# Side work of VectorE moved to other places of the iteration, two GpSimd operations behind a third, and the last stores cut by planes

## The chip, the cores and the metric

The kernel runs on one core of a Trainium2 chip. The metric is the device time of one execution in microseconds (us), as the median of three runs; lower is better. One execution was profiled besides, and the trace of it gives every instruction of the engines: TensorE (PE, its weight loads shown apart as PEld), VectorE (DVE), ScalarE (ACT), GpSimd (POOL) and SyncE (SP), which only issues DMAs here.

## The reference

A residual block of four modulated one-dimensional convolutions over x of 128 samples, 64 channels and 1024 positions, all in float32. For each sample and layer the weights are scaled by a style vector and normalised:

```python
def _layer(x, style, w, b, mw, mb, typ):
    s = style @ mw.T + mb
    weight = SCALE * w * s[:, None, :, None]
    demod = lax.rsqrt(jnp.sum(weight * weight, axis=(2, 3)) + EPS)
    weight = weight * demod[:, :, None, None]
    if typ == 'same':
        out = jax.vmap(_conv_same)(x, weight) + b[None, :, None]
    elif typ == 'upsample':
        out = jax.vmap(_conv_up)(x, weight.transpose(0, 2, 1, 3)) + b[None, :, None]
        out = _blur(out, 2.0 * blur_k, (1, 1))
    elif typ == 'downsample':
        xb = _blur(x, blur_k, (2, 2))
        out = jax.vmap(_conv_down)(xb, weight) + b[None, :, None]
    return out
...
for i, typ in enumerate(('same', 'upsample', 'same', 'downsample')):
    out = _layer(out, style, weights[i], biases[i], mod_w[i], mod_b[i], typ)
return x + out
```

## The kernel before

**The idea.** The four layers are linear in x, so for each sample they are one convolution of nine taps, a bias and a few samples at both ends that are computed apart. The kernel builds the composed weights of each sample on TensorE and then applies them with a fast algorithm: the nine taps are three groups of three, and the positions are stored as three planes (position modulo 3), so that five products of plane combinations with weight combinations give the three output planes.

**Groups and iterations.** The samples are taken four at a time: 32 groups, `NQ = 32`. The loop over `q` is a software pipeline; iteration q works on four groups at once: on q (its last products and its outputs), on n = q + 1 (its first products), on c = q + 2 (the last stages of its weights, its inputs) and on s = q + 3 (the first stage of its weights). All instructions are issued in the order written; each engine takes its own in that order, and semaphores hold back what is not ready.

**Weights.** `scale3`, `stage1` (split in `stage1_a` and `stage1_b`), `stage2` and `stage3` build the composed weights through the PSUM tiles psS, psR and psW. Each result is copied to SBUF by ScalarE with a factor per sample from a table: S with tB or tBn, R with tC, Wf with t0, wd with tA. Two parts of S are added up by VectorE from PSUM (L422), and GpSimd adds one part of S to another (L425, "the addition into S"). `combine_a` and `combine_b` form the weight combinations H from Wf on VectorE, SBUF to SBUF; between them `residual` adds the residual path, with the table t3.

**Inputs and products.** VectorE forms from X, the loaded planes, the tile G (`in_g01`, `in_g2`), then T3 (`in3`) and both T0 and T4 (`in04`); GpSimd forms T1 (`in1`, L566) and T2 (`in2`, L571) from G. TensorE makes the five products in `conv0` to `conv4`, twelve matmuls each, which the trace records as 24; conv0 to conv3 go into psA and conv4 into Y. `copy_m3` (ScalarE), `sum1` and `sum2` (VectorE, from PSUM) put them together between the products: sum1 reads psA behind conv1, and conv2 may only then write on in psA; sum2 reads psA behind conv2 and writes Y, and only then conv4 of the next iteration may add to Y. `output` scales a plane with td and adds tb, on ScalarE; `store` sends the planes from SP.

The order of VectorE in an iteration before the change is: sum2, combine_a, combine_b, T0/T4, T3, G, sum1, the additions into S, side work. That of GpSimd: T1, the addition into S, T2, side work. That of TensorE: psR, conv4, psW, conv3, psW, conv0 (first third), conv1 (first third), a slot or psS, conv1, conv0, psS, conv0, conv2. psR is thus the first work of an iteration.

**Side work.** The modulation of the samples beyond the first ones, their tables, the constants of the bias and the ends of the sequence are spread over the iterations by hand. `SLOTS` names the iterations in which TensorE makes a product for them, into psE, which ScalarE copies to `raw` ("slot iterations": 1, 2, 3, 5, 6, 7 small ones, and 9, 12, 14, 19, 24 with twelve matmuls for the ends); there `stage1_a` comes later. `EXTRA` names what follows on VectorE and GpSimd, by iteration and place: `var_root`, `var_inverse` (a reciprocal) and `var_newton` make the normalisation, `table_*` the tables, `vector_*` and `const_rest` the constants, `setup*`, `rest*` and `blur_side` the ends. Before the change both places, 0 and 1, are in the same spot, behind the additions into S.

**Buffers.** X and the T tiles have two buffers, G one, the weight tiles three or four; PSUM has two tiles for psA, one tile for psS, psR, psW and psE together, and one for Y.

Of the kernel before, what the change touches and what calls it, by code (L numbers as in the profile page):

```python
# [55 lines left out]
K = 3  # L56
# [7 lines left out]
def kernel(  # L64
# [9 lines left out]
    nc = tc.nc  # L74
    NP, P, NXC = x.shape
    B = 2 * NP
    NQ = B // 4
# [146 lines left out]
    def var_root(bs, src, ls=slice(0, NL)):  # L224
        src = by_layer(src, bs)[:, ls]
        nc_a.activation(nw[:, ls, bs], src, AF.Sqrt, bias=eps)
        nc_v.tensor_scalar(var[:, ls, bs], src, EPS, None, op0=ALU.add)
# [46 lines left out]
    def table_B(bs):  # L274
        table(nc_g, tB, bs, ALT, DOWN, sc[:, 2, bs], sc[:, 1, bs])

    def table_Bn(bs):
        qs = slice(bs.start // 4, bs.stop // 4)
        nc_g.tensor_scalar_mul(tBn[:, qs], tB[:, qs], -1.0)
# [429 lines left out]
    def vector_a1(bs):  # L709
        nc_g.tensor_mul(a1[:, bs], sc[:, 2, bs], sc[:, 1, bs])  # L710
# [318 lines left out]
    def var_and_constant(ps):  # L1029
# [11 lines left out]
        12: (ends1(0), HB * 5, HB * 5),  # L1041
        14: (ends1(1), HB * 4, HB * 4),
        19: (ends2, HB * 8, HB * 8),
        24: (ends3, HB * 3, HB * 3),
    }

    def after(side):
        return raw[turn[0]][:, side, :]

    def layers(i, j):  # L1050
        return REST, slice(i, j)
# [1 line left out]

    EXTRA = {
        (1, 1): lambda: const_rest(0, PART[1], after(0)),
        (2, 0): lambda: (table_B(REST), table_Bn(REST), vector_a1(REST)),
        (2, 1): lambda: (var_root(REST, after(0)), const_rest(1, PART[1], after(1))),
        (3, 0): lambda: (var_inverse(*layers(2, 3)), table_0(REST), vector_b1(REST)),
        (3, 1): lambda: (
            const_rest(2, PART[1], after(0)),  # L1060
            table_b(PART[1]),
            var_newton(*layers(2, 3)),
            var_inverse(*layers(1, 2)),
        ),
        (4, 0): lambda: (
            table_A(REST, dm[:, 2, REST]),
            var_inverse(*layers(0, 1)),
            var_newton(*layers(0, 2)),
            vector_c0(REST),
        ),  # L1070
        (4, 1): lambda: (table_C(REST), vector_c2(REST)),
        (5, 0): lambda: vector_Da(REST),
        (5, 1): lambda: (const_rest(0, REST, after(0)), var_inverse(*layers(3, 4))),
        (6, 0): lambda: (var_newton(*layers(3, 4)), table_3(REST), setup_x(0)),
        (6, 1): lambda: const_rest(1, REST, after(0)),
        (7, 0): lambda: setup_x(1),
        (7, 1): lambda: (const_rest(2, REST, after(0)), table_b(REST)),
        (8, 0): setup0,
        (9, 0): setup3,
        (9, 1): lambda: rest0(0),  # L1080
        (10, 0): lambda: rest0(1),
        (10, 1): lambda: setup1(0),
        (11, 0): lambda: setup1(1),
        (12, 1): lambda: rest1(0),
        (14, 1): lambda: rest1(1),
        (15, 0): lambda: rest1_bias(0),
        (16, 0): lambda: rest1_bias(1),
        (19, 1): lambda: rest2(0),
        (20, 0): lambda: rest2(1),
        (20, 1): lambda: blur_side(0, 0),  # L1090
        (21, 0): lambda: blur_side(1, 0),
        (21, 1): lambda: blur_side(0, 1),
        (22, 0): lambda: blur_side(1, 1),
        (22, 1): lambda: blur_side(0, 2),
        (23, 0): lambda: blur_side(1, 2),
        (24, 1): rest3,
        (25, 0): rest3_bias,
    }

    def extra(*at):  # L1100
# [2 lines left out]
    for q in range(NQ):  # L1103
        n, c, s = q + 1, q + 2, q + 3
        if q == 1:
            nc.sync.dma_start(Xe, x_ends)
        if q == 5:
            zeros()
        if n == NQ:
            conv4(q)  # L1110
            for i in range(2):
                output(q, 2, i)
            for i in range(2):
                output(q, 1, i, nc_v)
            for i in range(2):
                store(q, i, slice(1, 3))
            conv0(q, *range(K))
            for i, (eng, queue) in enumerate(zip(BOTH, (nc_a, nc.sync))):
                output(q, 0, i, eng)
                store(q, i, slice(0, 1), queue)  # L1120
            break
# [8 lines left out]
        if n == NQ - 1:  # L1130

            conv3(n, ps_w)
            copy_m3(n)
            conv4(q, 0, 1)
            for i in range(2):
                output(q, 1, i)
            conv1(n)
            sum1(n)
            conv4(q, 2)
            for i in range(2):  # L1140
                output(q, 2, i)
            in04(n, PAIR[0])
            in04(n, PAIR[1])
            conv0(q, 0)
            conv2(n)
            conv0(q, 1, 2)
            sum2(n)
            for i in range(2):
                output(q, 0, i)
                store(q, i)  # L1150
            continue

        conv4(q)
# [11 lines left out]
            stage3(c, 0)  # L1165
        conv3(n)
        copy_m3(n)
        in04(n)
        if q:
            in3(c)  # L1170
# [12 lines left out]
        if q:  # L1183
            in_g2(c)
            load(c + NX)
        later = q and c < NQ - 1
        if later:
            in1(c, nc_g)
        if n == NQ - 2:
            combine_a(n + 1, lambda: sum1(n))  # L1190
            combine_b(n + 1)
# [12 lines left out]
        conv2(n, 0)  # L1204
        if q in SLOTS:
            stage1_b(s)
        if later:
            in2(c, nc_g)
        extra(q, 0)
        extra(q, 1)  # L1210
        if s + 1 < NQ:
            scale3(s + 1)
        conv2(n, 1, 2)
# [86 lines left out]
```

## Time and profile before

| | us |
|---|---|
| median of 3 runs | 494.18 (494.17 to 494.41) |
| the profiled execution | 494.43 |
| its span, first to last instruction | 492.6 |
| granted TensorE clock, mean | 0.998 |
| PE busy | 480.1 |
| DVE busy | 406.0 |
| ACT busy | 290.3 |
| POOL busy | 141.9 |
| DMA, mean over the span | 143 GB/s |

The span is what the trace shows; the execution's own time is 1.8 us longer. Rows of a timeline give the start, the busy length, the engine, the line, the operation, what it writes and reads, its size, how many instructions were merged, and in brackets how long the engine was idle before and who ended that. A row of the chain of waits gives start, length and the instruction on the path that ended last. Adjoining operations of VectorE overlap by some 0.08 us in these records, and matmuls, whose ends are modelled, by some 0.2; the chain starts a group of matmuls at the end of the one before.

### The profile page before, as it was taken

What the parts mean: (1) busy time and instruction counts of PE and PEld (TensorE: products, weight loads), DVE (VectorE), ACT (ScalarE), POOL (GpSimd) and SP (SyncE); (2) the same over time, 40 slices, a digit from 0 to 9 for tenths busy, and PEclk for the clock granted to TensorE, in tenths of its full rate; (3) what the DMA queues carried; (4) which work ended last, traced back from release to release, by engine and by line L of the source; (5) the groups of instructions that cost most, each with busy time, mean ns of one, the idle gap of its engine ahead of it and who ended that gap; (6) DMA issues with size and microseconds to landing.
All of it is one profiled execution on the core that took longest, in us unless ns stands there. A gap on an engine that the chain in (4) does not pass through costs nothing.

```text
span 492.6 us, 22188 instructions
## 1 busy us (share of the span) xinstructions
PE 480.1 (97%) x10056; PEld 363.4 (74%) x10056; DVE 406.0 (82%) x632; ACT 290.3 (59%) x579; POOL 141.9 (29%) x175
## 2 busy tenths in 40 slices
PE   8999999999999999999999999999999999999995
PEld 6877787667767766777888888876777777777763
DVE  5986888898898969996769998759999869878783
ACT  5456646566556656556566656656566657556552
POOL 3544423434123232123232122232133332121200
PEclk9999999999999999999999999999999999999999
DMA  7220744442234442344532344442344442434224
GB/s 251 95 89 4 241 156 166 173 172 100 103 149 173 174 164 62 124 174 173 173 134 90 131 169 173 174 152 77 120 173 173 173 175 87 140 146 167 89 86 172
DMA packets 19727, 70.42 MB, mean 143 GB/s; under 512 B 2224, under 2 KB 2992, under 8 KB 19632
## 3 DMA queue, kind: packets, MB, share of 16 engines
q1 hardware_dynamic: 19408, 68.70, 38.4%
q8 instruction: 79, 1.29, 1.1%
q10 hardware_dynamic: 224, 0.29, 0.2%
q14 instruction: 16, 0.13, 0.1%
HBM read 35.36 MB, written 33.62 MB: 140 GB/s over the span
## 4 chain that ended last, share of the span: by engine, by line
PE 86%; DVE 9%; POOL 1%; issue 1%; ACT 1%; DVEq 0%
PE psA L593 40%; PE psW L480 14%; PE psR L439 12%; PE Y L593 11%; PE psS L369 5%; PE psE L823 2%; DVE Y L501 1%; DVE G L501 1%; PE Y L169 1%; DVE S L422 1%; ACT o L662 1%; DVE Ve L839 1%; PE Y L316 1%; DVE Ye L839 0%; DVE Ve L838 0%
## 5 line engine op out<-in xcount | busy, mean ns | idle before, releaser
L593 PE MATMUL psA<-T,H 64*64 64x340 f32 x2304 | 193.3, 446 | 0.6 <-DVE y L501 0.5
L593 PEld LDWEIGHTS psA<-T,H 64*64 64x64 f32 x2304 | 95.3, 133 | 51.1 <-issue 7.6
L566 POOL TENSOR_TENSOR T<-G 128x684 f32<-128x684 f32 x30 | 50.1, 1671 | 283.4 <-DVE G L501 251.5
L439 PE MATMUL psR<-S,E 64*64 64x192 f32 (+1 forms) x2304 | 87.6, 299 | 0.7 <-ACT S L340 0.4
L439 PEld LDWEIGHTS psR<-S,E 64*64 64x64 f32 x2304 | 80.8, 133 | 8.2 <-issue 1.0
L340 ACT ACTIVATE R<-psR,tC 128x448 f32<-128x448 f32 x63 | 36.6, 631 | 69.2 <-PE psR L439 67.4
L501 DVE SCALAR_TENSOR_TENSOR G<-X 128x1376 f32<-128x1376 f32 (+2 forms) x66 | 76.1, 1191 | 0.0
L593 PE MATMUL psA<-T,Wf 64*64 64x340 f32 x768 | 74.8, 447 | 0.0
L593 PE MATMUL Y<-T,Wf 64*64 64x340 f32 x768 | 62.2, 448 | 3.1 <-DVE Y L501 2.8
L340 ACT ACTIVATE Wf<-psW,t 128x384 f32<-128x384 f32 (+1 forms) x126 | 56.4, 498 | 12.2 <-PE psW L480 12.2
L480 PE MATMUL psW<-R,w0s 64*64 64x128 f32 (+1 forms) x1536 | 62.5, 287 | 0.4 <-ACT Wf L340 0.3
L501 DVE SCALAR_TENSOR_TENSOR y<-psA,m 128x680 f32<-128x680 f32 (+1 forms) x33 | 27.8, 845 | 37.8 <-PE psA L593 37.8
L480 PEld LDWEIGHTS psW<-R,w0s 64*64 64x64 f32 x1536 | 51.8, 133 | 7.8 <-ACT Wf L340 1.2
L662 ACT ACTIVATE o<-Y,tb,td 128x340 f32<-128x340 f32 x64 | 37.2, 631 | 27.7 <-ACT R L340 14.1
L571 POOL TENSOR_TENSOR T<-G 128x684 f32<-128x684 f32 x30 | 53.2, 1775 | 0.0
L580 DVE TENSOR_TENSOR T<-G 128x1368 f32<-128x1368 f32 (+1 forms) x33 | 50.5, 1534 | 0.0
L593 PEld LDWEIGHTS Y<-T,Wf 64*64 64x64 f32 x768 | 32.3, 133 | 20.9 <-DVE Y L501 6.0
L369 PEld LDWEIGHTS psS<-wd,w2n 64*64 64x64 f32 x1160 | 39.2, 133 | 10.3
L662 ACT ACTIVATE o<-psA,tb,td 128x340 f32<-128x340 f32 x63 | 36.7, 634 | 14.7 <-PE psA L593 14.7
L340 ACT ACTIVATE S<-psS,tBn 128x256 f32<-128x256 f32 x58 | 24.4, 471 | 25.7 <-PE psS L369 25.6
L625 ACT COPY m<-psA 128x680 f32<-128x680 f32 (+1 forms) x33 | 23.3, 710 | 25.6 <-PE psA L593 25.6
L662 ACT ACTIVATE o<-y,tb,td 128x340 f32<-128x340 f32 x62 | 38.1, 668 | 0.0
(147 smaller groups left out, 543.6 us busy)
## 6 DMA issues: line engine op xcount, KB each, us to landing
X<-in_x SPq DMA_DIRECT2D x64, 516.0 KB, 4.4
out<-o SPq DMA_DIRECT2D x62, 510.0 KB, 4.7
out<-o SPq DMA_DIRECT2D x2, 340.0 KB, 4.0
Xe<-in_x_ends SPq DMA_DIRECT2D x1, 512.0 KB, 7.9
par<-in_params SPq DMA_DIRECT2D x2, 192.0 KB, 3.4
par_s<-in_params_s SPq DMA_DIRECT2D x1, 196.0 KB, 2.7
par<-in_params SPq DMA_DIRECT2D x2, 96.0 KB, 2.7
out<-Oe SPq DMA_DIRECT2D x1, 192.0 KB, 3.1
```

The costliest lines, as they stand in the source:

```text
L340: nc_a.activation(dst, src, AF.Copy, scale=f)
L369: nc.tensor.matmul(ps[r][cols, at * C : (at + n) * C], weight[rows], wd[c if r == 0 else 1 - c][rows, taps], start=first, stop=last, skip_ ...
L439: nc.tensor.matmul(ps[r][cols, lo * C : (lo + m) * C], E[rows, e + 2, :], src[rows, a, :], start=(n == 0), stop=(n == 8), skip_group_check ...
L480: nc.tensor.matmul(ps[r][cols, at : at + m * C], w0s[kind][rows, k, :], rt[c][rows, first : first + K * (m - 1) + 1 : K, :], start=(n == 1 ...
L501: nc_v.scalar_tensor_tensor(out, x, f, y, op0=ALU.mult, op1=op)
L566: eng.tensor_add(t[:, :, 0, :NJ], plane(g, 2), plane(g, 1))
L571: eng.tensor_sub(t[:, :, 1, :NJ], plane(g, 2), plane(g, 1))
L580: nc_v.tensor_sub(t[:, pairs, :, :NJ], both(a, PL), both(b, 1))
L593: nc.tensor.matmul(ps[s][cols, :NB], w, Ts[q, tag][rows, c, i, g : g + NB], start=(g == 0 and m == 3), stop=(g == K - 1), skip_group_check ...
L625: nc_a.copy(m3c[q][:, s], a)
L662: nc_a.activation(dst, src, AF.Identity, bias=add, scale=d3)
L823: nc.tensor.matmul(ps[r][cols, : HB * n].rearrange("c (b j) -> c b j", j=n), weight(i, r, c)[rows], moving(i, r, c)[rows], start=(i == 0), ...
```

## The change

Three things are moved; apart from one `var_inverse` call that takes the place of two, no operation of the computation is added or left out.

1. The places 0, 1 and 2 of `EXTRA` are now at three spots: 0 ahead of T0/T4, 1 ahead of sum1 (in the last but one iteration ahead of combine_a), 2 where both were before, behind T2. All of VectorE's side work has gone to 0 and 1; tables and other GpSimd work that comes late stay at 2. The side work is also dealt out anew over the iterations, and slot 24 is now slot 25.
2. T1 (`in1`) is issued right ahead of T2, so on GpSimd both follow the addition into S.
3. In the last two iterations the stores are cut by planes: in iteration 30 planes 1 and 2 are stored ahead of plane 0; in iteration 31 plane 1 is made by VectorE ahead of conv4 in the issue order, and each plane has a store of its own, one of plane 1 and one of plane 0 from ScalarE's queue.

```diff
--- before.py
+++ after.py
@@ -1041,7 +1041,7 @@
         12: (ends1(0), HB * 5, HB * 5),
         14: (ends1(1), HB * 4, HB * 4),
         19: (ends2, HB * 8, HB * 8),
-        24: (ends3, HB * 3, HB * 3),
+        25: (ends3, HB * 3, HB * 3),
     }
 
     def after(side):
@@ -1053,48 +1053,37 @@
 
     EXTRA = {
         (1, 1): lambda: const_rest(0, PART[1], after(0)),
-        (2, 0): lambda: (table_B(REST), table_Bn(REST), vector_a1(REST)),
-        (2, 1): lambda: (var_root(REST, after(0)), const_rest(1, PART[1], after(1))),
-        (3, 0): lambda: (var_inverse(*layers(2, 3)), table_0(REST), vector_b1(REST)),
-        (3, 1): lambda: (
-            const_rest(2, PART[1], after(0)),
-            table_b(PART[1]),
-            var_newton(*layers(2, 3)),
-            var_inverse(*layers(1, 2)),
-        ),
-        (4, 0): lambda: (
-            table_A(REST, dm[:, 2, REST]),
-            var_inverse(*layers(0, 1)),
-            var_newton(*layers(0, 2)),
-            vector_c0(REST),
-        ),
-        (4, 1): lambda: (table_C(REST), vector_c2(REST)),
-        (5, 0): lambda: vector_Da(REST),
-        (5, 1): lambda: (const_rest(0, REST, after(0)), var_inverse(*layers(3, 4))),
-        (6, 0): lambda: (var_newton(*layers(3, 4)), table_3(REST), setup_x(0)),
-        (6, 1): lambda: const_rest(1, REST, after(0)),
-        (7, 0): lambda: setup_x(1),
-        (7, 1): lambda: (const_rest(2, REST, after(0)), table_b(REST)),
-        (8, 0): setup0,
-        (9, 0): setup3,
-        (9, 1): lambda: rest0(0),
-        (10, 0): lambda: rest0(1),
+        (2, 1): lambda: (const_rest(1, PART[1], after(1)), var_root(REST, after(0))),
+        (2, 2): lambda: (table_B(REST), table_Bn(REST), vector_a1(REST)),
+        (3, 0): lambda: (var_inverse(*layers(2, 3)), var_newton(*layers(2, 3))),
+        (3, 1): lambda: const_rest(2, PART[1], after(0)),
+        (3, 2): lambda: (table_b(PART[1]), table_0(REST), vector_b1(REST)),
+        (4, 0): lambda: (table_A(REST, dm[:, 2, REST]), var_inverse(*layers(0, 2))),
+        (5, 0): lambda: (var_newton(*layers(0, 2)), vector_c0(REST)),
+        (5, 1): lambda: const_rest(0, REST, after(0)),
+        (5, 2): lambda: (table_C(REST), vector_c2(REST), vector_Da(REST)),
+        (6, 0): lambda: (var_inverse(*layers(3, 4)), var_newton(*layers(3, 4))),
+        (6, 2): lambda: table_3(REST),
+        (7, 0): lambda: const_rest(1, REST, after(0)),
+        (7, 1): lambda: const_rest(2, REST, after(0)),
+        (7, 2): lambda: (table_b(REST), zeros()),
+        (8, 0): lambda: (setup_x(0), setup_x(1)),
+        (9, 0): lambda: (setup0(), setup3()),
+        (10, 0): lambda: rest0(0),
         (10, 1): lambda: setup1(0),
-        (11, 0): lambda: setup1(1),
-        (12, 1): lambda: rest1(0),
-        (14, 1): lambda: rest1(1),
-        (15, 0): lambda: rest1_bias(0),
-        (16, 0): lambda: rest1_bias(1),
-        (19, 1): lambda: rest2(0),
-        (20, 0): lambda: rest2(1),
-        (20, 1): lambda: blur_side(0, 0),
-        (21, 0): lambda: blur_side(1, 0),
-        (21, 1): lambda: blur_side(0, 1),
-        (22, 0): lambda: blur_side(1, 1),
-        (22, 1): lambda: blur_side(0, 2),
-        (23, 0): lambda: blur_side(1, 2),
-        (24, 1): rest3,
-        (25, 0): rest3_bias,
+        (11, 0): lambda: rest0(1),
+        (11, 1): lambda: setup1(1),
+        (13, 0): lambda: rest1(0),
+        (15, 0): lambda: rest1(1),
+        (16, 0): lambda: rest1_bias(0),
+        (17, 0): lambda: rest1_bias(1),
+        (20, 0): lambda: rest2(0),
+        (21, 0): lambda: rest2(1),
+        (22, 0): lambda: (blur_side(0, 0), blur_side(1, 0)),
+        (23, 0): lambda: (blur_side(0, 1), blur_side(1, 1)),
+        (24, 0): lambda: (blur_side(0, 2), blur_side(1, 2)),
+        (26, 0): rest3,
+        (27, 0): rest3_bias,
     }
 
     def extra(*at):
@@ -1104,16 +1093,14 @@
         n, c, s = q + 1, q + 2, q + 3
         if q == 1:
             nc.sync.dma_start(Xe, x_ends)
-        if q == 5:
-            zeros()
         if n == NQ:
+            for i, queue in enumerate((nc.sync, nc_a)):
+                output(q, 1, i, nc_v)
+                store(q, i, slice(1, 2), queue)
             conv4(q)
             for i in range(2):
                 output(q, 2, i)
-            for i in range(2):
-                output(q, 1, i, nc_v)
-            for i in range(2):
-                store(q, i, slice(1, 3))
+                store(q, i, slice(2, K))
             conv0(q, *range(K))
             for i, (eng, queue) in enumerate(zip(BOTH, (nc_a, nc.sync))):
                 output(q, 0, i, eng)
@@ -1139,6 +1126,7 @@
             conv4(q, 2)
             for i in range(2):
                 output(q, 2, i)
+                store(q, i, slice(1, K))
             in04(n, PAIR[0])
             in04(n, PAIR[1])
             conv0(q, 0)
@@ -1147,7 +1135,7 @@
             sum2(n)
             for i in range(2):
                 output(q, 0, i)
-                store(q, i)
+                store(q, i, slice(0, 1))
             continue
 
         conv4(q)
@@ -1165,6 +1153,7 @@
             stage3(c, 0)
         conv3(n)
         copy_m3(n)
+        extra(q, 0)
         in04(n)
         if q:
             in3(c)
@@ -1183,9 +1172,7 @@
         if q:
             in_g2(c)
             load(c + NX)
-        later = q and c < NQ - 1
-        if later:
-            in1(c, nc_g)
+        extra(q, 1)
         if n == NQ - 2:
             combine_a(n + 1, lambda: sum1(n))
             combine_b(n + 1)
@@ -1204,10 +1191,10 @@
         conv2(n, 0)
         if q in SLOTS:
             stage1_b(s)
-        if later:
+        if q and c < NQ - 1:
+            in1(c, nc_g)
             in2(c, nc_g)
-        extra(q, 0)
-        extra(q, 1)
+        extra(q, 2)
         if s + 1 < NQ:
             scale3(s + 1)
         conv2(n, 1, 2)
```

## The prediction

> **What bounds the kernel now.** I read the page first, then the chain of waits, then the timeline of single engines. Times are us from the span's start.
>
> ```profile
> span 492.6 us, 22188 instructions
> PE 86%; DVE 9%; POOL 1%; issue 1%; ACT 1%; DVEq 0%
> ```
>
> TensorE sets the end; VectorE stands on the chain for 9%. An iteration begins with the products into psR, so the distance from one psR to the next is its length (rows of the chain, two of a group of matmuls, one of a wait):
>
> ```profile
> 285.75 2.50 PE psR L439 x72
> 299.90 2.50 PE psR L439 x72
> 77.97 2.50 PE psR L439 x72
> 166.54 2.50 PE psR L439 x72
> 211.90 2.50 PE psR L439 x72
> 314.04 2.50 PE psR L439 x72
> 360.03 2.50 PE psR L439 x72
> 175.89 1.94 PE psE L823 x24
> 323.40 2.60 PE psE L823 x24
> L731 PE MATMUL psE<-cc,wsum 64*64 64x16 f32 (+1 forms) x16 | 1.1, 217 | 0.0
> 196.64 1.89 DVE Ye L839
> PEld Y L593 <- DVE Y L501: 6.0, 9, 1.1
> ```
>
> An undisturbed iteration takes 299.90 - 285.75 = 14.15. Iterations 3 to 8 take 88.57: six of 14.15 (84.90), four small slots of four matmuls each at 1.1/16 x 4 = 0.28 (1.1), and 2.6 more. Iterations 9 to 11 take 45.36 = 42.45 + 1.94 of slot + 1.0. Iterations 19 to 21 take 45.99 = 42.45 + 2.60 + 0.9. These **4.5 us** are conv4 waiting for sum2 (the weight load of Y waits 9 times for VectorE's Y), and in front of sum2 the chain shows side work such as Ye at 196.64.
>
> **What the moves save.** In the new order nothing but the two additions into S stands on VectorE between sum1 and sum2, so sum2 waits for TensorE alone, as here (sum2 at 314.09, 0.05 behind psR):
>
> ```profile
> 311.07 0.87 DVE L501 SCALAR_TENSOR_TENSOR y<-psA,m 128x680 f32<-128x680 f32 x1 [1.82 <-PE psA L593]
> 312.11 1.94 PE L593 MATMUL psA<-T,H 64*64 64x340 f32 x24
> 314.09 0.87 DVE L501 SCALAR_TENSOR_TENSOR Y<-m,psA 128x680 f32<-128x680 f32 x1 [1.64 <-PE psA L593]
> 60.12 0.80 PE L593 MATMUL psA<-T,H 64*64 64x340 f32 x8 [0.29 <-DVE y L501]
> 59.12 0.86 DVE L501 SCALAR_TENSOR_TENSOR y<-psA,m 128x680 f32<-128x680 f32 x1
> ```
>
> I count all 4.5 as saved. The floor is nothing, if what moves comes back in front of sum1.
>
> **What they cost in front of sum1.** Cover there is VectorE's idle 1.82 before sum1, plus 0.08 that adjoining operations overlap: 1.9. Beyond it conv2 waits at once: in iteration 1 conv2 starts 0.14 behind sum1's end (59.98 to 60.12), and in the steady one sum1's end 311.94 + 0.14 is 0.03 short of conv2 at 312.11. A slot iteration has about the same cover (1.8 to 1.9: sum1 comes earlier, but a longer group stands ahead of conv2); those with a psE of L823 have its 1.9 to 2.6 besides.
>
> The price of each operation where it ran undisturbed (its duration less 0.08 that the next one overlaps, plus 0.03 before one that needs its result):
>
> ```profile
> 92.39 0.37 DVE L759 TENSOR_TENSOR oc<-raw,dm 128x16 f32<-128x16 f32 x1
> 92.94 0.25 DVE L236 TENSOR_TENSOR nw<-dm,var 128x96 f32<-128x96 f32 x1
> 93.69 0.74 DVE L230 RECIPROCAL dm<-nw 128x96 f32<-128x96 f32 x1
> 183.58 0.56 DVE L838 TENSOR_TENSOR Ye<-raw,a 128x384 f32<-128x384 f32 x1
> 198.45 0.74 DVE L799 SCALAR_TENSOR_TENSOR g<-par,g 128x192 f32<-128x192 f32 x2
> 331.89 0.69 DVE L839 TENSOR_TENSOR Ve<-Ve,c 128x512 f32<-128x512 f32 x1
> ```
>
> A reciprocal costs 0.74 - 0.08 = 0.66, a const_rest of 16 columns 0.55 (92.39 to 92.94) and of 96 columns some 0.65, a Newton step of three operations 0.75 (92.94 to 93.69), half of rest0 1.1 (two of 0.56), half of setup1 0.65, half of rest2 1.3 (two of 0.69), half of setup_x 0.6 (one of the same 512 columns). A reciprocal of double width I take at twice the price, a Newton step at 1.1, both bounded above by two of the single ones.
>
> A second price is the **port**. VectorE and GpSimd hold each other up when both work SBUF to SBUF:
>
> ```profile
> 32.33 1.64 POOL L571 TENSOR_TENSOR T<-G 128x684 f32<-128x684 f32 x1
> 33.14 1.25 DVE L501 SCALAR_TENSOR_TENSOR H<-Wf 128x384 f32<-128x384 f32 x1
> 315.64 0.55 DVE L501 SCALAR_TENSOR_TENSOR H<-Wf 128x384 f32<-128x384 f32 x1
> 33.93 0.95 POOL L268 TENSOR_TENSOR tB<-sc 64x8 f32<-64x8 f32 x3
> 34.82 0.56 DVE L501 SCALAR_TENSOR_TENSOR H<-H,Wf 128x384 f32<-128x384 f32 x1
> 226.15 0.46 POOL L425 TENSOR_TENSOR S<-S 128x128 f32<-128x128 f32 x1 [2.55 <-ACT S L340]
> 227.72 2.50 PE psR L439 x72
> 281.58 0.84 ACT L340 ACTIVATE S<-psS,tBn 128x256 f32<-128x256 f32 x2 [1.02 <-PE psS L369]
> ```
>
> H took 1.25 where 0.55 is normal and ended 0.42 behind GpSimd's 33.97, which is 0.13 less than its own length. Both in1 and in2 now follow the addition into S. In slot iteration 12 that addition ends at 226.61; two operations of 1.64, each begun 0.04 early, end at 229.81. H is due 1.55 behind sum2 (314.09 to 315.64) and sum2 0.05 behind psR, at 229.32: 0.49 before GpSimd's end, less 0.13, is **0.35** after every slot. Without a slot S is ready at 282.42 in an iteration whose successor begins at 285.75: 0.46 for the addition and two of 1.64 end near 286.2, over 1 us before H is due (287.35). Sum1, sum2 and the additions into S on VectorE read PSUM and show their usual lengths beside GpSimd: free.
>
> In a slot iteration const_rest also waits for ScalarE's copy of psE, with sum1 queued behind it, and conv2 behind sum1. But two thirds of conv1 stand behind psE on TensorE and sum1 needs those, so the copy is there first: nothing, at most 0.3 in iteration 2, where var comes as well. ScalarE's nw moves there into a pause before S.
>
> Iteration by iteration: **1** has no idle before sum1 (59.12), so const_rest costs its whole 0.55. **3**: 0.66 + 0.75 + 0.55 + 0.35 = 2.3, over by 0.5. **4**: table_A some 0.4 (two operations of half the rows) and a reciprocal of double width 1.3, within 1.9. **5**: 1.1 + 0.65, within. **6**: 0.66 + 0.75 + 0.35, within, but table_C now stands behind in2 of slot 5: in2 ends 2.1 behind psR, its two operations take some 0.75 (three took 0.95), and R needs them:
>
> ```profile
> 125.00 1.16 ACT L340 ACTIVATE R<-psR,tC 128x448 f32<-128x448 f32 x2 [2.29 <-PE psR L439]
> 126.34 0.98 PEld L480 LDWEIGHTS psW<-R,par 64*64 64x64 f32 x24
> ```
>
> R is late by 0.3 to 0.5 and psW has 0.18 in hand (126.16 to 126.34): 0.3. Behind R on ScalarE stand plane 2 of the output and the copies into Wf, which shift with psW. **7**: t3 comes as late as table_C did, VectorE waits for it at residual, 0.85 late (due 2.1 behind psR, there at 2.95), with combine_b and T0/T4 behind; then 0.65 + 0.55: over by 0.15. **8**: 1.2 + 0.35, within. **10**: 1.1 + 0.65 + 0.35, over by 0.2. **11, 13, 15 to 17, 20 to 24, 26, 27**: at most 1.75, within. Sum **1.7**. Bounds: 0.5 (only iteration 1 pays) and 3.5 (all of these double). Slot 24 moves to 25 with its matmuls and its Oe store; nothing is added. Loads of X move by at most 1.8 with VectorE, two iterations ahead of their use.
>
> **Last stores.** Every store is one SP issue; the final ones:
>
> ```profile
> 487.50 0.38 ACTq L667 DMA_DIRECT2D out<-o  x1
> 483.80 4.12 SPq L667 DMA_DIRECT2D out<-o  x5
> out<-o SPq DMA_DIRECT2D x1, 170.0 KB, 4.0
> out<-Oe SPq DMA_DIRECT2D x1, 192.0 KB, 3.1
> 487.00:489.00 2.00, 0.00 (x0) 0.00 (x0) 0.53 (x1) 0.47 (x1) 0.00 (x0) 1.00 1.01 387
> ```
>
> From 487 to 489 the DMA engines are full (share 1.01): six stores of 2 x (510 + 340 + 170) KB are issued from 483.80 on. Now 680 KB of them go out some 3 us earlier, right behind plane 2 of iteration 30, and the other 1360 KB take 3.6 at 387 GB/s, so they are moved by 487.5, when the last two are issued. These then land like Oe, 3.1 instead of 4.0, less what the pair costs itself (0 to 0.45). I take **0.8**; bounds 0 and 1.6 (if the time falls with the bytes). ScalarE's new issue (0.38) waits for VectorE's y output, ahead of its own plane 2, which comes after conv4: covered.
>
> [...]
>
> Sum: the profiled execution took 494.43 (span 492.6 and 1.8 around it); 494.43 - 4.5 + 1.7 - 0.8 = 490.8. The median of the runs is 0.25 lower: **490.6**.
>
> **Rivals.** (a) *Slower: table operations hold the port too.* Tables now run on GpSimd right behind in2, beside H, in iterations 3, 4, 6, 7, 8 (5, 5, 4, 4, 2 operations). If each kept VectorE out for its 0.3, that is 6.0, less 0.6 already counted in 7 and 0.6 of spare in 4, 6 and 8: 4.8 more, **495.4**. It decides from 0.25 each on. Against it: in iteration 0 H at 34.82 took 0.56 beside such operations. The Trainium skill, SBUF — State Buffer, section Who interferes with whom, says that whichever starts first holds the pair for the whole instruction, which would make these block; iteration 0 does not bear that out for small ones.
> (b) *The port costs more than 0.35 after a slot* (H, then the residual held once more, as two operations in a row): 0.5 more in iterations 3, 6, 7, 10, which have no spare: **492.6**. For it: H lost 0.7 in iteration 0. Against it: it lost that to 0.83 of GpSimd's work ahead, as the price above assumes.
> (c) *Almost no cost:* sum1 in 3, 7, 10 and R stay inside unseen spare, only iteration 1 pays, stores give 1.6: 494.18 - 4.5 + 0.5 - 1.6 = **488.6**.
> (d) *The stores give nothing*, since a last store lands 4 behind its issue whatever stands ahead: **491.4**. Oe's 3.1 speaks against it.
>
> **Numbers.** Forecast 0.48 (its own range 489.7 to 491.3), (a) 0.12, (b) 0.20, (c) 0.12, (d) 0.08. A change under 0.2% (1.0) is no change a measurement here can tell. Faster: 0.48 + 0.12 + 0.08 + three quarters of (b) = 0.83; same: the rest of (b), 0.05; slower 0.12. Range 488.4 to 493.0: it leaves (a) out and holds the bounds of the stores and most of those in front of sum1.
>
> **What will show it.** Right: psR to psR 14.15 in iterations 4, 11 and 20 to 24; Y's weights no longer wait for VectorE; conv2 waits for y some 0.85 in iteration 1 and 0.5 in 3; R waits for tC in 6, Wf for t in 7; H near 0.9 after slots and 0.54 elsewhere; the last landing near 490 less the saved 2.8, with the span's final stretch 0.8 shorter. Wrong: conv2 waiting for y in more iterations than 1, 3, 7 and 10; H long beside tables; Y still waiting for VectorE; the final store still 4 behind its issue.

## The result, and the profile after

| | before | changed |
|---|---|---|
| median | 494.56 (494.17 to 494.86, 6 runs) | 490.44 (489.87 to 490.85, 6 runs) |
| profiled execution / its span | 494.43 / 492.6 | 490.55 / 488.8 |

The ratio is 0.9917 (95% interval 0.9904 to 0.993): faster by 4.1 us. The forecast was 490.6. Part of that closeness is luck, as the balance further down shows: a saving and its costs were both rated too low and offset each other, the stores gave next to nothing in the profiled execution, and two gaps went away that had not been in the sum.

The page of the changed kernel, the chain by engine:

```profile
span 488.8 us, 22191 instructions
PE 90%; DVE 6%; POOL 1%; issue 1%; ACT 1%; DVEq 0%
```

VectorE's share of the chain fell from 9 to 6%. The chain of waits of the changed kernel, the rows that begin an iteration (start, length, what):

```profile
62.85 2.50 PE psR L439 x72
92.86 2.50 PE psR L439 x72
107.01 2.50 PE psR L439 x72
...
164.71 2.50 PE psR L439 x72
...
209.37 2.50 PE psR L439 x72
...
311.51 2.50 PE psR L439 x72
...
356.58 2.50 PE psR L439 x72
```

Iteration 4 now takes 107.01 - 92.86 = 14.15, the undisturbed length. Iterations 9 to 11 take 209.37 - 164.71 = 44.66 instead of 45.36, iterations 19 to 21 take 356.58 - 311.51 = 45.07 instead of 45.99. The waits of the changed kernel (who waited for whom: us in total, times, longest):

```profile
DVE Y L501 <- PE psA L593: 34.3, 29, 1.6
ACT R L340 <- POOL tC L268: 4.7, 2, 2.9
PE psA L593 <- DVE y L501: 1.3, 3, 0.6
```

In 29 iterations sum2 waits for TensorE (8 before), and the weight load of Y no longer appears as waiting for VectorE. In its place conv2 waits for sum1 three times. Two of these three, the wait of R and one of Wf stand in the timelines of TensorE, ScalarE and VectorE (start, duration, operation, and in brackets the idle time before it and who ended it):

```profile
60.67 0.80 PE L593 MATMUL psA<-T,H 64*64 64x340 f32 x8 [0.59 <-DVE y L501]
90.68 0.80 PE L593 MATMUL psA<-T,H 64*64 64x340 f32 x8 [0.43 <-DVE y L501]
124.47 0.63 ACT L340 ACTIVATE R<-psR,tC 128x448 f32<-128x448 f32 x1 [2.87 <-POOL tC L268]
139.20 0.48 DVE L498 SCALAR_TENSOR_TENSOR Wf<-idn,t,Wf 128x64 f32<-128x64 f32 x2 [0.58 <-POOL t L268]
```

These are iterations 1, 3, 6 and 7, four of the five places that the prediction named; in the fifth, iteration 10, the chain gives 14.44 (180.79 to 195.23). VectorE's rows of iteration 3 show what stands ahead of sum1 there:

```profile
79.57 0.90 DVE L501 SCALAR_TENSOR_TENSOR H<-Wf 128x384 f32<-128x384 f32 x1
81.42 0.63 DVE L501 SCALAR_TENSOR_TENSOR H<-Wf 128x384 f32<-128x384 f32 x1
...
89.33 0.17 DVE L759 TENSOR_TENSOR oc<-raw,dm 128x16 f32<-128x16 f32 x1
...
89.68 0.86 DVE L501 SCALAR_TENSOR_TENSOR y<-psA,m 128x680 f32<-128x680 f32 x1
```

The first H takes 0.90 instead of 0.55 behind GpSimd's in2: 0.35, the port's price to the hundredth. But const_rest of 16 columns takes 89.68 - 89.33 = 0.35, not 0.55, and two later H take 0.63, 0.08 more than usual, beside the tables on GpSimd.

The stores are the term that this profile does not show. The prediction had named a final store still 4 behind its issue as a sign of being wrong, and this profile has it. The last one, in the table of DMA issues of the final stretch (queue, count, size, us from issue to landing):

```profile
out<-o SPq DMA_DIRECT2D x1, 170.0 KB, 4.1
```

And the stretch before its landing, in the table of stretches (length, busy time of PE, PEld, DVE, ACT, POOL, PE's clock, DMA share, GB/s):

```profile
484.00:486.00 2.00, 0.00 (x0) 0.00 (x0) 0.00 (x0) 0.00 (x0) 0.00 (x0) 1.00 1.00 207
```

The final landing is 4.1 behind its issue, as late as before (4.0), and the DMA engines are full at only 207 GB/s, where they moved 387 in the stretch that the prediction quotes. What the stores are worth is shown only by the further runs below.

### The profile page after: what moved, and what is told of

It reads as the page before. It is cut to its first block, busy times and chain, and to the rows that moved or that the text cites. A ratio compares the mean times of both kernels' runs of the same rounds, so it can differ in the third digit from the quotient of the medians.

```text
span 488.8 us, 22191 instructions
## 1 busy us (share of the span) xinstructions
PE 478.8 (98%) x10056; PEld 379.9 (78%) x10056; DVE 385.4 (79%) x631; ACT 289.9 (59%) x579; POOL 142.8 (29%) x175
## 4 chain that ended last, share of the span: by engine, by line
PE 90%; DVE 6%; POOL 1%; issue 1%; ACT 1%; DVEq 0%
PE psA L593 42%; PE psR L439 15%; PE psW L480 14%; PE Y L593 10%; PE psS L369 5%; PE psE L823 2%; DVE G L501 2%; DVE H L501 1%; PE Y L169 1%; DVE T L580 1%; PE Y L316 1%; DVE y L501 0%; DVE Wf L498 0%; DVE Y L501 0%; POOL T L566 0%
## 5 line engine op out<-in xcount | busy, mean ns | idle before, releaser
L593 PE MATMUL psA<-T,H 64*64 64x340 f32 x2304 | 195.6, 447 | 1.3 <-DVE y L501 1.3
L593 PEld LDWEIGHTS psA<-T,H 64*64 64x64 f32 x2304 | 102.4, 133 | 46.2 <-issue 14.5
L425 POOL TENSOR_TENSOR S<-S 128x128 f32<-128x128 f32 x29 | 13.5, 465 | 283.8 <-ACT S L340 283.8
L593 PE MATMUL psA<-T,Wf 64*64 64x340 f32 x768 | 76.5, 447 | 0.0
L480 PEld LDWEIGHTS psW<-R,w0s 64*64 64x64 f32 x1536 | 54.1, 133 | 6.5 <-ACT Wf L340 1.2
L501 DVE SCALAR_TENSOR_TENSOR Y<-m,psA 128x680 f32<-128x680 f32 (+1 forms) x33 | 28.0, 849 | 34.8 <-PE psA L593 34.3
L566 POOL TENSOR_TENSOR T<-G 128x684 f32<-128x684 f32 x30 | 50.3, 1678 | 15.5 <-DVE G L501 15.5
L571 POOL TENSOR_TENSOR T<-G 128x684 f32<-128x684 f32 x30 | 49.9, 1662 | 0.0
L369 PEld LDWEIGHTS psS<-wd,w2n 64*64 64x64 f32 x1160 | 40.9, 133 | 8.6
L593 PEld LDWEIGHTS Y<-T,Wf 64*64 64x64 f32 x768 | 36.0, 133 | 12.7 <-issue 0.6
L501 DVE SCALAR_TENSOR_TENSOR H<-Wf 128x384 f32<-128x384 f32 x64 | 39.5, 617 | 0.0
```

The source lines that it names most:

```text
L369: nc.tensor.matmul(ps[r][cols, at * C : (at + n) * C], weight[rows], wd[c if r == 0 else 1 - c][rows, taps], start=first, stop=last, skip_ ...
L425: nc_g.tensor_add(t[:, :, 2], t[:, :, 2], t[:, :, 0])
L480: nc.tensor.matmul(ps[r][cols, at : at + m * C], w0s[kind][rows, k, :], rt[c][rows, first : first + K * (m - 1) + 1 : K, :], start=(n == 1 ...
L501: nc_v.scalar_tensor_tensor(out, x, f, y, op0=ALU.mult, op1=op)
L566: eng.tensor_add(t[:, :, 0, :NJ], plane(g, 2), plane(g, 1))
L571: eng.tensor_sub(t[:, :, 1, :NJ], plane(g, 2), plane(g, 1))
```

## The experiments

The kernels were run in series: a series is a few kernels run in turn on one chip, the kernel before among them. All ratios are to the kernel before in the same series.

### The stores alone, and the change without them

The first kernel is the kernel before with the cut stores only, the second the changed kernel with the old stores:

```
 penultimate iteration, after output(q, 2, i):   + store(q, i, slice(1, K))
 and at its end:                                 - store(q, i)   + store(q, i, slice(0, 1))
 last iteration, ahead of conv4:                 + output(q, 1, i, nc_v); store(q, i, slice(1, 2), queue)
 and behind it:                                  - output(q, 1, i, nc_v)
                                                 - store(q, i, slice(1, 3))   + store(q, i, slice(2, K))
```

> The kernel before with the third part of the change alone, the last stores by planes. The prediction's term (the last two stores land 3.1 instead of 4.0 behind their issue) gives 0.8 less, 493.8 beside 494.6, and a last landing 3.1 to 3.5 behind the last issue. The rival, that the stores give nothing, gives 494.6 and a landing some 4.1 behind the last issue, as the changed kernel's trace has it (issue 483.74, landing 487.86).

> The changed kernel with the last stores as they were before. If the cut stores give nothing, this stays at the changed kernel's 490.4 (within 0.3); if they gave the 0.8 of the prediction, and something else lost it, 491.2. Last landing some 4.0 behind the last issue in either case.

The stores alone: 493.05 (492.45 to 495.71, 8 runs), 0.9974 [0.9958, 0.9991], the kernel before at 494.94 in that series. The change without them: 491.29 (491.14 to 491.6), 0.9933 [0.9918, 0.9947]. So the stores gave 0.0026 of the time by the one and 0.9933 - 0.9917 = 0.0016 by the other (there across two series, with intervals that overlap), 1.3 and 0.8 us. The last store by the table of DMA issues, first with the stores alone, then in the change without them, and the stretch from 484 to 486 of the latter:

```profile
out<-o SPq DMA_DIRECT2D x1, 170.0 KB, 3.3
```

```profile
out<-o SPq DMA_DIRECT2D x1, 170.0 KB, 4.5
```

```profile
484.00:486.00 2.00, 0.00 (x0) 0.00 (x0) 0.00 (x0) 0.00 (x0) 0.00 (x0) 0.79 0.99 371
```

With the old stores the same stretch moves 371 GB/s, far more than the 207 above, and the last store still lands later: more was left to move.

### GpSimd's T1 ahead of the addition again

The changed kernel, with T1 put back ahead of the addition into S (T2 stood behind it before the change too):

```
+        if q and c < NQ - 1:
+            in1(c, nc_g)
         (ahead of combine_a, as in the kernel before)
-            in1(c, nc_g)
             in2(c, nc_g)
```

> The changed kernel with T1 back ahead of the addition into S on GpSimd. If the port is what the move of T1 is for, T1 now starts as soon as G is there and runs beside the side work between G and sum1: the second operation of const_rest or setup1 waits for T1's end (about 1.4 later) in iterations 1, 3, 5, 7, 10 and 11, sum1 and conv2 with it, while H after a slot is short again (0.55 instead of 0.90): 5 to 8 us more in all, 495 to 498, and rows of L764, L760 or L799 at 1.5 or more. If the port plays no part there: 490.4 with all these at 0.2 to 0.4.

Measured: 494.36 (493.45 to 495.91, 10 runs), 0.9987 [0.9976, 0.9999]: 0.0070 above the changed kernel's ratio, or 3.5 us, where 5 to 8 had been expected. The move of the side work without that of T1, the cut stores included, thus gains 0.0013, no more than the 0.0026 of the stores alone. What it does is seen in the timelines of iteration 11, a row each of VectorE, GpSimd and TensorE:

```profile
210.71 2.12 DVE L799 SCALAR_TENSOR_TENSOR g<-par,g 128x192 f32<-128x192 f32 x2
210.97 1.65 POOL L566 TENSOR_TENSOR T<-G 128x684 f32<-128x684 f32 x1 [11.54 <-DVE G L501]
213.76 0.52 PE L593 MATMUL psA<-T,H 64*64 64x340 f32 x4 [0.95 <-DVE y L501]
```

GpSimd's T1 starts as soon as G is there. The two operations of setup1 at L799 stand on VectorE at that moment, and take 2.12; in the changed kernel, with T1 behind the addition, the same two take 0.75. They are held up for 1.37, sum1 is late by that less what cover was left, and conv2 waits 0.95. In iterations 3, 5, 7 and 10 it is the same with const_rest or setup1: conv2 waits 1.45, 0.94, 0.37 and 0.96. Iteration 6 gets 0.4 back (14.39), since T1's earlier end lets table_C come in time for R. Iteration 1, which had been expected to lose as well, keeps its 15.46: there T1 starts only at 61.80, when the two operations of const_rest (61.58 and 61.78) are all but done.

### T1 behind the addition, and nothing else

The kernel before, with that one move:

```
-        if later:
-            in1(c, nc_g)
         ...
+            in1(c, nc_g)
             in2(c, nc_g)
```

> The kernel before with the second part of the change alone, T1 behind the addition into S, while the side work stays behind sum1. By the port, side work after a slot now meets T1 and then T2 instead of T2 alone, up to 1.6 more ahead of sum2 in the iterations after slots, of which the cover of conv4 takes a part: 5 to 11 us more, 500 to 506. If the three parts work independently: 494.6, or less if T1's place by itself saved something.

Measured: 509.09 (508.17 to 510.36, 4 runs), 1.0293 [1.0271, 1.0315]: 14 us slower, more than expected. The timelines of this kernel, iteration 7 on VectorE, GpSimd and TensorE (where conv4 begins), and const_rest on VectorE in iteration 8:

```profile
141.42 1.59 DVE L237 SCALAR_TENSOR_TENSOR nw<-nw,dm 128x96 f32<-128x96 f32 x1
...
141.22 1.67 POOL L571 TENSOR_TENSOR T<-G 128x684 f32<-128x684 f32 x1
...
145.40 0.96 PE L593 MATMUL Y<-T,Wf 64*64 64x340 f32 x8 [2.14 <-DVE Y L501]
...
160.17 1.69 DVE L759 TENSOR_TENSOR oc<-raw,dm 128x96 f32<-128x96 f32 x1
```

An operation of the Newton step, 0.26 long elsewhere, takes 1.59 while GpSimd makes an input, conv4 waits 2.14 for the late sum2, and the const_rest of 96 columns 1.69, where 0.25 is its length in the kernel before. So the two halves of the change are one: T1 behind the addition fills the stretch from sum1 to sum2 with GpSimd's SBUF work, which pays only when VectorE has none there, and T1 ahead of it meets the side work that now stands before sum1.

### The price of the table steps on GpSimd

The changed kernel, with table and vector steps of slots (2, 2) and (3, 2) issued three times (the same values again):

```
-        (2, 2): lambda: (table_B(REST), table_Bn(REST), vector_a1(REST)),
+        (2, 2): lambda: [(table_B(REST), table_Bn(REST), vector_a1(REST)) for _ in range(3)],
-        (3, 2): lambda: (table_b(PART[1]), table_0(REST), vector_b1(REST)),
+        (3, 2): lambda: (table_b(PART[1]), [(table_0(REST), vector_b1(REST)) for _ in range(3)]),
```

> The changed kernel with the GpSimd table and vector steps of slots (2,2) and (3,2) issued three times (same values again): some ten more small GpSimd operations in the slot of iteration 3 and six in that of iteration 4. The prediction's price (such an operation costs VectorE 0.05 to 0.08): iteration 3 grows by 0.5 to 0.8 us, from 14.9 to 15.4 to 15.7, iteration 4 by 0.3 to 0.5. Rival (each holds VectorE for its whole length, about 0.3): iteration 3 grows by 3.0 us, iteration 4 by 1.8. Rival (nothing beside GpSimd's small operations costs anything): no growth.

One execution, 489.96. The timelines of iteration 3 behind H, on GpSimd, VectorE and TensorE (conv2):

```profile
87.08 1.55 POOL L279 TENSOR_SCALAR tBn<-tB 128x48 f32<-128x48 f32 x1
...
84.31 1.68 DVE L580 TENSOR_TENSOR T<-G 128x1368 f32<-128x1368 f32 x1
...
89.17 0.35 DVE L759 TENSOR_TENSOR oc<-raw,dm 128x16 f32<-128x16 f32 x1
90.70 0.52 PE L593 MATMUL psA<-T,H 64*64 64x340 f32 x4 [0.99 <-DVE y L501]
```

Conv2 waits 0.99 instead of 0.43: ten more operations cost 0.56, 0.06 each, where holding VectorE for their length would have cost 3.0. (The price of 0.05 to 0.08 named in the expectation is not in the prediction, which left it out; it is what the H of iteration 3 lost in the changed kernel.) It is GpSimd that waits: tBn takes 1.55 beside VectorE's G (there from 86.78 to 89.24), where it took 0.52 beside H, and VectorE's take 0.07 to 0.18 more (T 1.68 instead of 1.58, the first operation of const_rest 0.35 instead of 0.17). Iteration 4 keeps its 14.15, where 0.3 to 0.5 more had been expected: the cover there takes what the six more cost.

The row of oc explains a figure of the prediction: const_rest had been priced by an oc of 0.37, and that is its length with GpSimd beside it: in the kernel before, GpSimd's T2 stood there from 91.08 to 92.73.

### The cover ahead of the first sum

The changed kernel, with setup_x(0) three times more in iteration 18 and four times more in iteration 28, ahead of T0/T4:

```
+        (18, 0): lambda: [setup_x(0) for _ in range(3)],
+        (28, 0): lambda: [setup_x(0) for _ in range(4)],
```

> The changed kernel with the 512-column setup step (0.61 us from start to start) issued three times more ahead of T0/T4 in iteration 18 (1.83 us) and four times more in iteration 28 (2.44 us). The prediction's cover of 1.9 us before the first sum: iteration 18 keeps 14.14 to 14.17, iteration 28 grows by about 0.5 to 14.6 to 14.7. Rival (no cover, each step delays the first sum): they grow by 1.8 and 2.4. Rival (the cover is larger than worked out): both keep 14.14 to 14.17.

One execution, 491.02. The timeline of VectorE in 18 and in 28, and that of TensorE in 28 (conv2):

```profile
301.80 2.13 DVE L803 TENSOR_TENSOR Xm<-Xe,sc 128x512 f32<-128x512 f32 x3
303.85 1.58 DVE L580 TENSOR_TENSOR T<-G 128x1368 f32<-128x1368 f32 x1
...
447.45 2.86 DVE L803 TENSOR_TENSOR Xm<-Xe,sc 128x512 f32<-128x512 f32 x4
450.23 1.58 DVE L580 TENSOR_TENSOR T<-G 128x1368 f32<-128x1368 f32 x1
452.51 2.63 DVE L501 SCALAR_TENSOR_TENSOR G<-X 128x1376 f32<-128x1376 f32 x2
...
456.06 0.80 PE L593 MATMUL psA<-T,H 64*64 64x340 f32 x8 [0.89 <-DVE y L501]
```

The steps are longer than they had been taken for, presumably since each rewrites the same tile and waits for the one before (the two of iteration 8, which write different halves, begin 0.60 apart): 303.85 - 301.80 = 2.05 for three and 450.23 - 447.45 = 2.78 for four. By the chain, iteration 18 takes 14.26 (297.09 to 311.35), 0.12 more than the undisturbed length, where 2.05 - 1.9 is 0.15. Iterations 27 and 28 take 29.41 (428.60 to 458.01), 1.13 more than two undisturbed ones. In 28 VectorE is so late that its G meets GpSimd's addition into S (there from 453.64 to 454.41), and G takes 2.63 instead of 2.37: 2.78 + 0.26 - 1.9 is 1.14. So in these two iterations the cover is 1.9 to within 0.03, and what goes beyond it is paid in full. The growths expected, 0 and 0.5, were off by the length of the step and by this meeting.

### The side work spread once more

The changed kernel with the five steps that had cost something put elsewhere, and the changed kernel again beside it:

```
-        (1, 1): lambda: const_rest(0, PART[1], after(0)),
+        (2, 0): lambda: const_rest(0, PART[1], after(0)),
 (2, 2): + var_inverse(*layers(2, 3))      (3, 0): - var_inverse(*layers(2, 3))
 (5, 0): + table_C(REST)                   (5, 2): - table_C(REST)
 (5, 2): + var_inverse(*layers(3, 4))      (6, 0): - var_inverse(*layers(3, 4))
 (9, 0): + setup1(0)                       (10, 1): - setup1(0)
```

> The changed kernel with five of its side steps put elsewhere: the rest of const for PART1 from (1,1) to (2,0), var_inverse(2,3) from (3,0) to (2,2), the rest of table_C from (5,2) to (5,0), var_inverse(3,4) from (6,0) to (5,2), setup1(0) from (10,1) to (9,0). Theory (each cost of the prediction belongs to its own slot and goes when that slot is relieved): iteration 1 loses its 0.30, iteration 3 its 0.5 to 0.63, iteration 6 its 0.35, iteration 10 its 0.29, some 1.5 us in sum, so about 488.9 beside 490.4 for the changed kernel. Rival (the work only moves its cost along, to iterations 2, 5 and 9): 490.0 to 490.6.

> The changed kernel itself, beside the others on the same chip: about 490.4, ratio near 0.992 to the kernel before; its last store lands 3.1 to 4.1 us after its issue. If the landing of 4.1 us in its first profile was chance, this one is nearer to 3.3.

The respread kernel: 489.5 (489.12 to 490.36, 6 runs), 0.9899 [0.9877, 0.992]; the changed one 490.05 (489.75 to 490.53, 6 runs), 0.9909 [0.989, 0.9928]. That is 0.55 us, with intervals that overlap, against 1.5 expected. The chain of the respread kernel, the rows that begin an iteration, and then its last store in the table of DMA issues:

```profile
62.97 2.50 PE psR L439 x72
106.44 2.50 PE psR L439 x72
149.61 2.50 PE psR L439 x72
...
253.69 2.50 PE psR L439 x72
268.19 2.50 PE psR L439 x72
```

```profile
out<-o SPq DMA_DIRECT2D x1, 170.0 KB, 4.3
```

Against the first profile of the changed kernel, iterations 2 to 4 take 43.47 instead of 44.16, 5 to 7 take 43.17 instead of 43.56 (107.01 to 150.57 there), iteration 10 takes 14.14 (179.84 to 193.98) instead of 14.44 (180.79 to 195.23), and conv2 in iteration 1 waits 0.28 instead of 0.59: 1.7 in sum, some 0.2 of it from iteration 2, whose length differs from profile to profile anyhow. Each cost went when its slot was relieved, all but some 0.1 in iteration 6; iteration 4 takes 14.28, 0.13 more than in the changed kernel. But iteration 15, which the edit does not touch, takes 14.50 instead of 14.15, and the last landing is 4.3 behind its issue (3.3 in the changed kernel beside it). The next runs ask whether these two belong to it.

### Which of the cut stores gives the gain

Three kernels on one chip: the respread kernel with both cuts, the same with only the early cut (planes 1 and 2 of iteration 30 ahead of its plane 0), and the same with only the last iteration's planes one by one.

> The kernel with the five side steps elsewhere, again, with both cuts, beside the two others: 489.5, 0.5 to 0.6 below the changed kernel. Its first profile lost 0.39 in iteration 15 and its last store landed 4.33 us after its issue; if these two were chance, iteration 15 is 14.18 here, the landing 3.1 to 3.6, and the profiled time 488.6 to 489.2. Theory (what shifts by itself is that profile): that. Rival (the respread causes both): 14.56 and 4.3 again.

> The kernel with the five side steps elsewhere (489.5), of whose cut stores only the early ones are left: planes 1 and 2 of iteration 30 still go out ahead of its plane 0, while those of the last iteration go out as before the change. Theory (the gain is the 680 KB that leave early, as the prediction put it): nearly all of the cut's 0.8 to 1.3 stays, so 489.4 to 489.8. Rival (the gain is the last iteration's planes, issued one by one): 490.3 to 490.8.

> The same, the other way round: iteration 30 stores all three planes at its end, as before the change, and only the last iteration's planes go out one by one, plane 1 ahead of conv4. Theory (the early 680 KB make the gain): 490.3 to 490.8. Rival (the last planes make it): 489.4 to 489.8.

| | median | ratio, 95% |
|---|---|---|
| both cuts | 488.42 (488.01 to 488.73, 4 runs) | 0.9875 [0.9856, 0.9895] |
| the early cut only | 488.75 (487.89 to 489.72, 5 runs) | 0.9888 [0.9869, 0.9906] |
| the last planes only | 490.10 (489.47 to 490.64, 5 runs) | 0.9912 [0.9896, 0.9927] |

Without the early cut the kernel loses 1.7 us (490.10 - 488.42), without the last one 0.3, which lies within the intervals. So the 680 KB that leave early make the gain, as the prediction had it. With both cuts the median is 1.1 below that of the series before, the kernel before 0.27 (494.28 and 494.01), so the three stand lower than expected, at the distances expected. The last stores by the table of DMA issues, in the order of the three kernels (both issues of SP's together in the third):

```profile
out<-o SPq DMA_DIRECT2D x1, 170.0 KB, 3.2
```

```profile
out<-o SPq DMA_DIRECT2D x1, 170.0 KB, 3.4
```

```profile
out<-o SPq DMA_DIRECT2D x2, 170.0 KB, 4.1
```

In nine profiles with the early cut, the last store landed 3.1 to 3.6 behind its issue in seven, and 4.1 and 4.3 in two; the kernels of these two were profiled again and had 3.3 and 3.2. In the profiles without it, the landing was 4.0 or more. So the long landing of the changed kernel's first profile is something that comes and goes. The end of the profiles says the same of the gain: from the start of TensorE's last group of matmuls (484.89 in the kernel before, of a span of 492.6) to the end of the span it takes 7.7 to 8.3 in the four profiles without the early cut, 6.7 to 7.1 in the seven, and 7.7 and 7.9 in the two with a late landing. Over all nine that is 0.9 less on average, and the last planes alone take 8.1, so they gain nothing there. Iteration 15 does not come and go: with both cuts again it takes 14.51 (253.67 to 268.18). Its sum1 begins some 0.4 later than in the changed kernel, although the matmuls of conv1 stand at the same distance from the beginning of the iteration in both profiles. What holds sum1 there was not found, and no run tried it.

The respread kernel is the fastest one seen, 0.9875 and 0.9899 in its two series, against 0.9909 and 0.9917 for the changed kernel in its own. For what the respread is worth the estimates run from the 0.55 us of the one series to 1.7 across two (0.9909 - 0.9875). The profiles have 1.2 less from the beginning of iteration 1 to that of iteration 29 (409.64 in the changed kernel, 408.42 and 408.46 in the respread one).

## Why the prediction was right

The profiled time fell by 494.43 - 490.55 = 3.9, where 3.6 had been forecast against it. The steps of the sum, one by one:

| step | predicted | measured |
|---|---|---|
| conv4 no longer waits for sum2 | -4.5 | -5.0 |
| iteration 1 | +0.55 | +0.30 |
| iteration 3 | +0.5 | +0.6 |
| iteration 6 | +0.3 | +0.5 |
| iteration 7 | +0.15 | +0.14 |
| iteration 10 | +0.2 | +0.3 |
| last stores | -0.8 | 0 to -0.1 in the profile, -0.8 to -1.7 in timed runs |

*What the moves save.* Of the 4.5, 0.9 lay in iterations 19 to 21, where nothing was to be paid: 45.99 - 45.07 = 0.92 came back. In 9 to 11 it was 1.0 less 0.2; 0.70 came. In 3 to 8 it was 2.6 less 0.95. Iterations 2 to 8 (62.30 to 166.54 before, 62.85 to 164.71 after) gained 2.38, and 0.52 of this is a gap of TensorE in iteration 2 of the profile before, which the prediction had not in its sum. The chain of the kernel before has it:

```profile
67.05 0.52 issue
...
418.07 2.50 PE psR L439 x72
...
432.55 2.50 PE psR L439 x72
```

Without it 1.86 remain, for 1.65 forecast. So the three stretches gave 3.48, where 4.5 less 1.15 of cost is 3.35. With the 1.5 that was paid in them, as the rows below show, it makes 5.0. TensorE's rows that begin iterations 5 to 8 of the changed kernel, from its timeline (iteration 3 goes from 77.77 to 92.65 there):

```profile
106.80 2.71 PE L439 MATMUL psR<-S,E 64*64 64x192 f32 x72
121.11 2.69 PE L439 MATMUL psR<-S,E 64*64 64x192 f32 x72
135.91 2.69 PE L439 MATMUL psR<-S,E 64*64 64x192 f32 x72
150.36 2.71 PE L439 MATMUL psR<-S,E 64*64 64x192 f32 x72
```

Iteration 5, whose side work the forecast had within the cover, takes 121.11 - 106.80 = 14.31. Its slot thus adds 0.16, and that of iteration 3 adds 0.12 at most (14.26 in the respread kernel, 77.69 to 91.95). The prediction had set aside 0.28 for each small slot: that is the mean busy length of the matmuls of two shapes, four times over, and these overlap their neighbours. So the four slots of iterations 3 to 8 take 0.6 and not 1.1, and the 0.5 between was conv4 waiting for sum2 as well. The saving was rated too low by 0.5 and the costs in these stretches by 0.4, so that the net came out right: this is luck.

That sum2 must be alone behind sum1 for this is shown by the kernel with T1's move alone, and its other half by the kernel with T1 ahead.

*The prices ahead of sum1.* They were 1.7 in sum and came to 1.8: TensorE's lengths less 14.15 and the slot are 14.88, 14.80 and 14.45 less 14.27, 14.31 and 14.31 in iterations 3, 6 and 7, and 0.3 each in 1 (beside the kernel before) and 10. The cover of 1.9 was right, and is the figure that did most work. The port's 0.35 was right. The undisturbed price of const_rest was not: 0.55 had been worked out from rows beside GpSimd's work, and 0.3 to 0.35 is what two operations of 16 columns cost alone. In iteration 1 this is the whole difference. In iteration 3 it is outweighed by two things that the forecast left out: the tables cost VectorE some 0.15 in passing, and the reciprocal and the Newton step behind it take 1.54 (83.23 to 84.77 on VectorE) where 1.41 had been taken. So its 0.5 is near in sum and not in its parts. Iteration 7's wait of Wf for t came as forecast (0.58); the list of waits shows none of conv2 there, but the iteration is 0.14 longer than iteration 5 with its like slot. In iteration 6 R came 124.47 - 121.11 = 3.36 behind the beginning of the iteration, 2.77 before the change: 0.6 late, where 0.3 to 0.5 had been forecast. The kernel that made table_C earlier got most of it back (14.42).

*The stores.* The mechanism was right: it is the early 680 KB. The size is known within a factor of two: 0.8 had been forecast, and the runs have 1.3 by the stores alone, 0.8 by the change without them, 1.7 by the last comparison and 0.9 by the ends of the profiles. No row shows the upper bound of 1.6. The landing of 3.1 to 3.6 in seven of nine profiles was near the 3.1 forecast, but the row that this came from was no fixed price: the store of Oe itself landed in 1.8 in every kernel that has the slot at 25, so that the fit is in part luck. The first profile of the changed kernel, with 4.1, would have led to the opposite verdict if taken by itself.

*The balance.* From iteration 0 to TensorE's last matmul the profiles show 4.1 less (455.03 and 450.96), where -4.5 + 1.7 gave 2.8. The rest of 1.3 is 0.25 in iteration 1, 0.13 in the three stretches, the 0.52 of iteration 2, and 0.34 in iteration 26, which took 432.55 - 418.07 = 14.48 before and 14.14 after. Iteration 0 then began 0.25 later (31.34 and 31.59), and the stores gave 0.1 in that execution. So the 3.9 of the profile and the 3.6 of the forecast are near each other partly because gaps that nobody had counted on stood in for the stores.

*The rivals.* (a), tables that hold VectorE for their length, falls: 0.06 for each, not 0.3. The Trainium skill, SBUF — State Buffer, section Who interferes with whom, has the engine that starts first hold the pair for its whole instruction. For long operations the traces agree (const_rest at 1.69 beside GpSimd's inputs, tBn at 1.55 beside VectorE's G); for small ones on GpSimd they put a far lower price on VectorE than their length. (b), a second operation held after a slot, is not there: the residual behind sum2 keeps its 0.86, and H loses once. (c), almost no cost, falls with 1.8 measured. (d), stores that give nothing, looks true in one profile and is refuted by the timed runs.

## What to carry to other kernels

A stretch between two dependent sums should hold, on the engine that makes them, nothing that a second engine's SBUF work can hold up: freeing that stretch and letting the other engine fill it is one change, and the second half alone cost 14 us here. Work out the cover ahead of the next wait from one undisturbed iteration, fill it and no more; here that figure held to 0.03 us in the two iterations where it was loaded on purpose. Take the length of what a slot adds from an iteration with nothing else in it, not from the busy time of its matmuls. Price an operation from a row with nothing beside it, and judge the last stores by timed runs, since their landing varies by a microsecond between executions of one kernel.

## What the runs showed that was not expected

- Small GpSimd operations beside long ones of VectorE wait themselves (a TENSOR_SCALAR of 128x48 at 1.55 instead of 0.52) and cost VectorE 0.06 each.
- In the two profiles whose last store landed late, the full DMA engines moved only 207 GB/s (changed kernel, 484 to 486) and 205 (respread kernel, 482 to 484, share 0.99). With the same stores the changed kernel moved 288 at a share of 0.83 the second time, and the kernel with the last planes alone 371 at 0.99. So the low rate is not the price of cutting the stores by planes; it comes and goes with the late landing, and its cause is open.
- Gaps of TensorE of 0.3 to 0.5 come and go in iterations whose own code is not changed: in 2 and 26 before, in 15 with the respread side work, there in every profile taken. Edits elsewhere move them, and their cause is open.
